# Edge matrix counted in steps of two tiles by 28 destination nodes, with the tile, degree and counting work pinned to the text's order

## Chip, cores and metric

The kernel runs on one core of one Trainium2 chip. The metric is the device time of one execution in microseconds (us), as the median of several runs. The engines are named as in the profile: PE (TensorE: matmuls, with PEld for their weight loads), DVE (VectorE), ACT (ScalarE), POOL (GpSimd) and SP (SyncE, which here only issues DMAs).

## What is computed

A graph of 6250 nodes and 100000 edges, sorted by destination `dst`, goes through two graph networks, each followed by a residual sum and a layer norm. Cut to what matters:

```
# network 0: three relational layers (R = 8 edge types, 128 features)
for l in range(3):
    h   = einsum('ni,rio->nro', x, weight[l])          # a message per node and type
    msg = h[src, etype] / max(count[dst, etype], 1)
    x   = segment_sum(msg, dst) + x @ root[l] + bias[l]
    if l < 2: x = relu(batch_norm(x))
x = layernorm(x_in + x)

# network 1: three steps of propagation over the same edges (64 features)
h = x @ W_in + b_in ;  deg = edges per src ;  dis = deg**-0.5 (0 where deg is 0)
acc = cur = h
for _ in range(3):
    cur = segment_sum(cur[dst] * dis[src] * dis[dst], src)
    acc = acc + cur
out = layernorm(x + (acc / 4) @ W_out + b_out)
```

## The kernel before, in words

**Gather stage.** The sorted edges form 782 tiles of 128. For each tile `one_sum` (L1046) lets POOL gather 128 message rows of 512 B by an indirect DMA (L1048) into one of 27 buffers `gt`, and PE multiplies them by a one-hot matrix `o` (L1051), which DVE makes for eight tiles at a time (`one_hots`, L1040 and L1042). `joined` lets DVE add a finished sum from PSUM into `agg` (L1630) or, for the low destinations, into `z` (L1079). Of each layer's 782 tiles, 92 are left to a dense product (`dense_sums`); 100 are gathered from node rows (`first_sums`, table `x_d`) and 590 from message rows (`window_sums`, table `h_d`): 690 gathers for each of three layers, 2070 in all. Between two layers stand a batch norm (L1674 to L1694), the writing of the new `x_d`, and 49 blocks of messages (`messages`, L953 to L958: PE, ACT, a DMA to `h_d`), which go on beside the next layer's first gathers.

**Side work.** Network 1 needs the number of edges between each pair of nodes, as a matrix, and the degrees. This is worked out beside the gathers by a generator, `side_work` (L1588), with N_SIDE steps: `hot_counts` (a small matrix for the low destinations), `degrees` (four tiles a step), and then `counts`. `take_turns` (L1615) moves the generator on in proportion to the gathered tiles: N_SIDE steps in TURNS = 1460 turns. With the code's constants N_SIDE is 1263, so a turn has 0.865 steps. No turn is taken in the dense stretch, in the first 66 tiles of layers 1 and 2 (the first 100 of layer 0), or in the last QUIET = 24 tiles of layers 0 and 1; after a batch norm FILL = 16 steps are put in at once (L1695).

**Counting.** `counts` (L1427) first lays out 245 steps: each holds four tiles whose destinations fall into one block of 128. It copies each step's edges into tables by one-hot matmuls (L1506). Then, for each of 980 tiles, DVE makes `row` (L1564), 1152 columns wide, with the value 16^field in the column of the edge's source, and, for four tiles at once, `dst_hot` (L1560), the one-hot of the destination. PE multiplies them into three PSUM banks of the pool `ps_w`, which has five (512, 512 and 128 columns, L1577; stationary `dst_hot`, moving `row`). Three instructions of `leave` (L1535) add the sum to that of the step before and store it as integers in `had`. SP writes `had` (576 KB) to the DRAM matrix `a_d` if the step is the last of its block (L1546, a conditional DMA).

**Last stage.** Network 1 (from L1711) reads `a_d` three times, in loads of 448 KB (L1829). DVE splits the nibbles (L1831, L1832), and PE multiplies by the features: 7203 matmuls (L1837).

**What sets the order.** A scheduler orders the instructions of each engine when the program is built. It goes by priorities from the text and by a model of durations, so an engine's order can differ from the text's. On the chip each engine runs its own order in sequence and waits on semaphores.

Of the kernel before, what the change touches and what calls it, by code (L numbers as in the profile page):

```python
# [519 lines left out]
def sorted_path(  # L520
# [34 lines left out]

    nc = tc.nc
# [48 lines left out]
    NG4 = Q * J // TS  # L605
    NST = NG4 + NBLK
# [6 lines left out]
    assert T1 + AND <= HT and P1 == 2 and W == 4 * P1 * P and 15 * NS1 <= NST * TS  # L613
    assert D == P and N * R <= 1 << 16 and R == 8 and H == 64
    assert 96 < Q <= P and N + P <= PAD and NBLK % CH == 0 and J == 2 * TS and NST <= 256
# [124 lines left out]
    b_out_r = const.tile([P, D], F32, name="b_out_r")  # L740

# [294 lines left out]
    def one_hots(column, share, width, t, end):  # L1036

        n = min(GPB, end - t)
        o = op.tile([P, GPB, HC], F32, name="o")
        nc.vector.tensor_tensor(o[:, :n, :width], iota_f[:, None, :width].to_broadcast([P, n, width]),  # L1040
                                column[:, t : t + n, None].to_broadcast([P, n, width]), op=OP.is_equal)
        nc.vector.tensor_tensor(o[:, :n, :width], o[:, :n, :width],  # L1042
                                share[:, t : t + n, None].to_broadcast([P, n, width]), op=OP.mult)
        return o

    def one_sum(pa, table, at, o, t, first_, last):  # L1046
        gt = gp.tile([P, D], F32, name="gt")
        nc.gpsimd.indirect_dma_start(  # L1048
            out=gt, out_offset=None, in_=table[:, :],
            in_offset=bass.IndirectOffsetOnAxis(ap=at[:, t : t + 1], axis=0))  # L1050
        nc.tensor.matmul(pa, gt, o, start=first_, stop=last)  # L1051
# [19 lines left out]
    def first_sums(l, nodes, steps, tiles, side):  # L1071
# [3 lines left out]
        def joined(t, pa):  # L1075
# [3 lines left out]
            nc.vector.tensor_add(to, to, pa.rearrange("p (d r) -> p d r", r=R))  # L1079
# [34 lines left out]
    ac = tc.alloc_tile_pool(name="ac", bufs=3)  # L1114
# [4 lines left out]
    a_d = dram.tile([NSL, P, NBLK, P], I32, name="a_d")  # L1119
    iota_c = kp.tile([P, S], mybir.dt.int16, name="iota_c")  # L1120
    nc.gpsimd.iota(iota_c, pattern=[[1, S]], base=0, channel_multiplier=0)
# [4 lines left out]
    nc.gpsimd.iota(iota_q, pattern=[[0, 1]], base=0, channel_multiplier=2,  # L1126
                   allow_small_or_imprecise_dtypes=True)

    e_src, e_rel, rel_s, e_val = (kp.tile([P, NST, TS], F32, name=f"e_tab{k}") for k in range(4))
# [10 lines left out]
    def hot_counts():  # L1140
# [130 lines left out]
        had = ac.tile([P, S], I32, name="had")  # L1271
        nc.vector.memset(had[:, :SR], 0)
        made, sums, at = {}, {}, {}
        for i in range(NS1 + 2):
            if i < NS1:
                hot = cp.tile([P, TS, P], BF16, name="dst_hot")
                nc.vector.tensor_tensor(hot[:, :P1, :], iota_f[:, None, :].to_broadcast([P, P1, P]),
                                        e_lo[:, i, :, None].to_broadcast([P, P1, P]), op=OP.is_equal)
                rows = []
                for j in range(P1):  # L1280
                    row = rp.tile([P, S], BF16, name="row")
                    nc.vector.tensor_scalar(row[:, :SR], iota_c[:, :SR], e_col[:, i, j : j + 1],
                                            e_v[:, i, j : j + 1], op0=OP.is_equal, op1=OP.mult)
# [3 lines left out]
            if 0 <= s < NS1:  # L1287
                hot, rows = made.pop(s)
                sums[s] = ps_w.tile([P, 512], F32, name="pw")
                for j in range(P1):  # L1290
                    nc.tensor.matmul(sums[s][:, :SR], hot[:, j, :], rows[j][:, :SR], start=(j == 0),
                                     stop=(j == P1 - 1))
            s = i - 2
            if s >= 0:
                now = ac.tile([P, S], I32, name="had")
                nc.vector.scalar_tensor_tensor(now[:, :SR], had[:, :SR], keep[:, s : s + 1],
                                               sums.pop(s)[:, :SR], op0=OP.mult, op1=OP.add)
# [7 lines left out]
                nc.sync.dma_start(c1_d[:, bass.ds(at[0, s], 1), :], now[:, None, :SR], cond=(at[1, s] == 1))  # L1305
# [82 lines left out]
    def degrees():  # L1388
# [9 lines left out]
        for t0 in range(0, NTS + TS, TS):  # L1398
            n = min(TS, NTS - t0)
            if n > 0:  # L1400
                hot = cp.tile([P, TS, P], BF16, name="lo_hot")
                blk = cp.tile([P, TS, NBLK], BF16, name="blk_hot")
                nc.vector.tensor_tensor(hot[:, :n, :], iota_f[:, None, :].to_broadcast([P, n, P]),  # L1403
                                        src_lo[:, t0 : t0 + n, None].to_broadcast([P, n, P]),
                                        op=OP.is_equal)
                nc.vector.tensor_tensor(blk[:, :n, :],
                                        iota_f[:, None, :NBLK].to_broadcast([P, n, NBLK]),
                                        src_blk[:, t0 : t0 + n, None].to_broadcast([P, n, NBLK]),
                                        op=OP.is_equal)
                made[t0] = hot, blk, n  # L1410
            if t0:
                hot, blk, n = made.pop(t0 - TS)
                for j in range(n):
                    t = t0 - TS + j
                    nc.tensor.matmul(pd, hot[:, j, :], blk[:, j, :], start=(t == 0), stop=(t == NTS - 1))  # L1415
# [11 lines left out]
    def counts():  # L1427

        B = NBLK
        edge = kp.tile([P, B], F32, name="edge")  # L1430
        nc.vector.tensor_scalar(edge, iota_f[:, :B], float(P), None, op0=OP.mult)
        d_in = dst_f[:, 1 : W + 1]
        p_t = [ps_w.tile([P, 512], F32, name="pw")[:B, :1] for _ in range(2)]
        for h in range(2):
            below = [cp.tile([Q, B], F32, name=f"below{k}") for k in range(2)]
            nc.vector.tensor_scalar(below[0], edge[:Q, :], d_in[:, h * 512 + 511 : h * 512 + 512], None,
                                    op0=OP.is_gt)
            nc.vector.tensor_scalar(below[1], edge[:Q, :], float(P), d_in[:, h * 512 : h * 512 + 1],
                                    op0=OP.add, op1=OP.is_gt)
            for k in range(2):  # L1440
                nc.tensor.matmul(p_t[k], below[k], ones[:Q, :1], start=(h == 0), stop=(h == 1))
        col = kp.tile([B, 8], F32, name="col")
        t0, n, incl, s0, delta, pos, top = (col[:, i : i + 1] for i in range(7))
        nc.vector.tensor_copy(t0, p_t[0])
# [477 lines left out]
```

## Time and profile before

| what | value |
|---|---|
| median of 11 runs | 3674.63 us (3664.24 to 3683.68) |
| the profiled execution's own time | 3665.64 us |
| its span, first to last instruction | 3663.9 us |
| busy: PE / DVE / POOL / ACT | 2889.7 / 2449.0 / 2152.0 / 321.1 us |
| DMA packets, bytes | 274421, 373.10 MB |
| last gather of layer 0; first gather of layer 1 | ends at 1026.5; starts at 1067.3 us |
| last gather of layer 2 | ends at 2968.8 us |
| last stage, L1837 | 7203 matmuls, 614.5 us busy |

Read it with the stages in mind: a share of the span is an average over stages with different limits. A group's line gives line, engine, operation, output<-input, shapes and count; behind the first bar the busy time and the mean of one in ns; behind the second the idle time of the engine just before them and what ended it. A line of a stretch gives, for each engine, the busy time in that stretch and, in brackets, the number of instructions, then the granted clock of PE, the DMA share and GB/s.

### The profile page before, as it was taken

The numbers are of one execution on the slowest core, as the hardware profiler recorded it, in microseconds if no ns is written. First come the engines' busy times: TensorE is split into PE (matmuls) and PEld (weight loads), VectorE is DVE, ScalarE is ACT, GpSimd is POOL, SyncE is SP. The second block draws the span as 40 slices with busy tenths as digits, with TensorE's granted clock in tenths as the row PEclk, the third lists the DMA queues.
The fourth block names the chain that finished last, engine by engine and source line by source line (L and its number), as shares of the span: only waits on it lengthen the run. The fifth ranks groups of instructions, "written<-read, shape, count | busy, mean of one in ns | idle before, by whom it ended". The sixth has DMA issues, their size and how long they took to land.

```text
span 3663.9 us, 51372 instructions
## 1 busy us (share of the span) xinstructions
PE 2889.7 (79%) x17520; PEld 2038.6 (56%) x17520; DVE 2449.0 (67%) x6315; ACT 321.1 (9%) x600; POOL 2152.0 (59%) x2083
## 2 busy tenths in 40 slices
PE   5865555687769878887767797787778769999998
PEld 3454444454444544444444454444445459999997
DVE  7667777873771688788548437878884557555555
ACT  3500000000016000000000340000001020000000
POOL 6677877777646777777766557777777730000000
PEclk9955555687769777677777897767878669999999
DMA  6611122233138222222422662222334224545442
GB/s 199 220 48 50 50 55 58 60 80 81 46 93 320 55 63 63 64 70 70 98 63 67 213 229 73 78 73 80 83 83 100 71 92 134 161 137 153 136 136 68
DMA packets 274421, 373.10 MB, mean 102 GB/s; under 512 B 86718, under 2 KB 197726, under 8 KB 274148
## 3 DMA queue, kind: packets, MB, share of 16 engines
q1 hardware_dynamic: 199464, 230.31, 20.0%
q0 software_dynamic: 66240, 135.79, 14.2%
q10 hardware_dynamic: 8444, 3.61, 0.4%
q8 instruction: 140, 2.29, 0.3%
q14 instruction: 133, 1.09, 0.1%
HBM read 250.74 MB, written 243.64 MB: 135 GB/s over the span
## 4 chain that ended last, share of the span: by engine, by line
PE 52%; DVE 25%; DMA 12%; issue 8%; POOL 2%; DVEq 1%; ACT 0%; POOLq 0%; ACTq 0%; SPq 0%
PE pw L1837 15%; PE ps L1051 12%; DMA gt<-h_d,gidx 10%; PE pw L1577 10%; DVE row L1564 6%; PE pw L956 6%; DVE had L1535 6%; PE pw L1352 3%; DVE agg L1630 2%; DVE o L1040 2%; POOL gt L1048 2%; PE pw L1379 1%; PE pw L969 1%; DVE dst_hot L1560 1%; DVE lo_hot L1403 1%
## 5 line engine op out<-in xcount | busy, mean ns | idle before, releaser
L1048 POOL DMA_INDIRECT gt<-h_d,gidx x1770 | 1830.5, 1034 | 561.7 <-issue 205.4
L1577 PE MATMUL pw<-row,dst_hot 128*128 128x128 bf16 (+1 forms) x2940 | 856.3, 418 | 298.7 <-DVE row L1564 146.1
L1051 PEld LDWEIGHTS ps<-o,gt 128*128 128x128 f32 x4140 | 781.4, 265 | 452.3 <-DMA gt<-h_d,gidx 189.3
L1051 PE MATMUL ps<-o,gt 128*128 128x48 f32 (+1 forms) x4140 | 811.0, 346 | 253.5 <-DMA gt<-h_d,gidx 155.5
L1564 DVE TENSOR_SCALAR row<-iota_c,e_tab,e_tab 128x1152 bf16<-128x1152 int16 x980 | 571.2, 591 | 280.2 <-PE pw L1577 278.6
L1577 PEld LDWEIGHTS <-dst_hot 128*128 128x128 bf16 x2940 | 340.5, 128 | 692.4 <-issue 610.5
L1837 PE MATMUL pw<-three,u 128*128 128x193 bf16 x7203 | 614.5, 248 | 14.4 <-DVE three L1764 10.1
L1837 PEld LDWEIGHTS <-u 128*128 128x128 fp8e3 x7203 | 601.3, 98 | 21.7 <-DVE three L1764 10.2
L1535 DVE SCALAR_TENSOR_TENSOR had<-had,keep,pw 128x128 int32<-128x128 int32 x735 | 444.0, 605 | 0.0
L1048 POOL DMA_INDIRECT gt<-x_d,xidx x200 | 195.8, 979 | 187.3 <-PE ps L1051 66.8
L956 PE MATMUL pw<-w,xT 128*128 128x512 f32 x588 | 285.8, 622 | 1.8 <-ACT hs L957 1.7
L1831 DVE TENSOR_SCALAR u<-packed 128x896 int32<-128x896 int32 x189 | 117.8, 624 | 194.2 <-PE pw L1837 194.1
L1403 DVE TENSOR_TENSOR lo_hot<-iota_f,e_tab 128x512 bf16<-128x512 f32 x196 | 134.7, 687 | 101.6 <-PE pd L1415 101.6
L1630 DVE TENSOR_TENSOR agg<-agg,ps 128x48 f32 x885 | 174.9, 198 | 32.0 <-PE ps L1051 26.7
L957 ACT COPY hs<-pw 128x512 f32<-128x512 f32 x294 | 168.7, 586 | 175.7 <-PE pw L956 144.3
L1040 DVE TENSOR_TENSOR o<-iota_f,lo 128x384 f32<-128x384 f32 x222 | 121.9, 549 | 87.7 <-PE ps L1051 87.6
L1352 PE MATMUL pw<-x,u 128*128 128x385 bf16 x735 | 169.1, 369 | 0.7 <-DVE x L1345 0.7
L1560 DVE TENSOR_TENSOR dst_hot<-iota_f,e_tab 128x512 bf16<-128x512 f32 x245 | 167.5, 684 | 0.0
L1048 POOL DMA_INDIRECT gt<-in_x_dram,xidx x100 | 122.7, 1227 | 67.8 <-PE ps L1051 37.5
L956 PEld LDWEIGHTS pw<-w,xT 128*128 128x128 f32 x588 | 106.8, 197 | 99.6 <-issue 80.9
L1079 DVE TENSOR_TENSOR z<-z,ps 128x56 f32 x300 | 61.9, 206 | 145.3 <-PE ps L1051 135.8
L1352 PEld LDWEIGHTS <-u 128*128 128x128 fp8e3 x882 | 97.4, 113 | 72.8 <-issue 29.5
(398 smaller groups left out, 1830.3 us busy)
## 6 DMA issues: line engine op xcount, KB each, us to landing
a_d<-had SPq DMA_DIRECT2D x245, 576.0 KB
packed<-a_d SPq DMA_DIRECT2D x189, 448.0 KB
h_d<-hs SPq DMA_DIRECT2D x147, 512.0 KB
gt<-h_d,gidx POOLq DMA_INDIRECT x1770
c_d<-had SPq DMA_DIRECT2D x62, 196.0 KB
packed<-c_d SPq DMA_DIRECT2D x21, 448.0 KB
x_d<-xc SPq DMA_DIRECT2D x24, 256.0 KB
xc<-in_x_dram SPq DMA_DIRECT2D x19, 256.0 KB
```

The lines of the kernel that those rows point to most:

```text
L956: nc.tensor.matmul(ph, xT[:, b * P : (b + 1) * P], w[:, c : c + 512], start=True, stop=True)
L1040: nc.vector.tensor_tensor(o[:, :n, :width], iota_f[:, None, :width].to_broadcast([P, n, width]), column[:, t : t + n, None].to_broadcast([ ...
L1048: nc.gpsimd.indirect_dma_start(out=gt, out_offset=None, in_=table[:, :], in_offset=bass.IndirectOffsetOnAxis(ap=at[:, t : t + 1], axis=0))
L1051: nc.tensor.matmul(pa, gt, o, start=first_, stop=last)
L1352: nc.tensor.matmul(sums[d][:, :C3D], us[d % 2][:, i, :, d // 2], x3[:, i, :], start=(c == 0 and i == 0), stop=(c * CH + i == NBLK - 1))
L1403: nc.vector.tensor_tensor(hot[:, :n, :], iota_f[:, None, :].to_broadcast([P, n, P]), src_lo[:, t0 : t0 + n, None].to_broadcast([P, n, P]), ...
L1535: nc.vector.scalar_tensor_tensor(now[:, c : c + w], had[:, c : c + w], keep[:, s : s + 1], p[:, :w], op0=OP.mult, op1=OP.add)
L1560: nc.vector.tensor_tensor(hots[s], iota_f[:, None, :].to_broadcast([P, TS, P]), rel_s[:, s, :, None].to_broadcast([P, TS, P]), op=OP.is_equal)
L1564: nc.vector.tensor_scalar(rows[i], iota_c, e_src[:, s, j : j + 1], e_val[:, s, j : j + 1], op0=OP.is_equal, op1=OP.mult)
L1577: nc.tensor.matmul(p[:, :w], hots[s][:, j, :], row[:, c : c + w], start=(j == 0), stop=(j == TS - 1))
L1630: nc.vector.tensor_add(to, to, pa)
L1837: nc.tensor.matmul(out_of(f), bytes_[f % 2][:, d, :, f // 2], cur[:, order[c0 + d], :], start=(c0 + d == 0 and f % 2 == 0), stop=(c0 + d = ...
```

## The change

**The counting step.** A step now holds two tiles (TU) whose destinations fall into one block of 28 nodes (DB); there are 224 such blocks (NDB), hence 616 steps and 1232 tiles. Stationary and moving operand change places. `row` is 252 columns wide (28 destinations by 9 residues of the source's block) and is the stationary side, in two halves of 126; the moving side is a one-hot of the source's place in its block of 128. So a tile needs two matmuls of 128 columns, a step one PSUM bank (126 x 256), one instruction in `leave`, and a write of 126 KB if it is the last of its block. N_SIDE becomes 1516 (1.038 steps a turn). The pools of `row` and `had` take smaller tiles; `had` has five buffers and not three.

**The tables** in `counts` are laid out for 616 steps, with twice as many one-hot matmuls of 308 columns, and for 224 blocks, in two halves of 112.

**The order.** `pin` ties an instruction to the one pinned before it on the same engine, without a semaphore: the scheduler must keep the text's order among them. Pinned are the one-hots `o`, the gather matmuls, the sums of `joined`, and the one-hots, rows, matmuls and `had` of hot_counts, degrees and counts. The rest stays free: messages, batch norm, dense sums, table building, DMAs.

**The last stage** reads the matrix in its new layout: per load one residue of block numbers (6 or 5 blocks), 512 B in a piece and not 3584 B: 243 loads, not 189, of 384 or 320 KB. The matmuls are as many and as large as before.

```diff
     TS = 4
-    NG4 = Q * J // TS
-    NST = NG4 + NBLK
+    TU = 2
+    DB = 28
+    NDB = NP // DB
+    HB = DB * NSL // 2
+    NST = Q * J // TU + NDB
...
+    in_turn = {}
+
+    def pin(ins):
+
+        last = in_turn.get(ins.ins.engine)
+        if last is not None:
+            tc.add_manual_dep(ins.ins, last.name,
+                              mybir.DependencyInfo(mybir.DependencyClass.NoSync, mybir.DependencyReason.DATA),
+                              reason="order of turns")
+        in_turn[ins.ins.engine] = ins.ins
...
-        nc.tensor.matmul(pa, gt, o, start=first_, stop=last)
+        pin(nc.tensor.matmul(pa, gt, o, start=first_, stop=last))
...
-    ac = tc.alloc_tile_pool(name="ac", bufs=3)
+    ac = tc.alloc_tile_pool(name="ac", bufs=5)
...
-    a_d = dram.tile([NSL, P, NBLK, P], I32, name="a_d")
+    a_d = dram.tile([NDB, 2 * HB, P], I32, name="a_d")
...
-                nc.tensor.matmul(pd, hot[:, j, :], blk[:, j, :], start=(t == 0), stop=(t == NTS - 1))
+                pin(nc.tensor.matmul(pd, hot[:, j, :], blk[:, j, :], start=(t == 0), stop=(t == NTS - 1)))
...
-            for j in range(TS):
-                pe = ps_w.tile([P, 512], F32, name="pw")
-                for h in range(2):
-                    c = h * 512 + j * P
-                    nc.tensor.matmul(pe[:, :NST], of[:, c : c + P], sel[h], start=(h == 0), stop=(h == 1))
-                nc.vector.tensor_copy(to[:, :, j], pe[:, :NST])
+            for j in range(TU):
+                for x0 in range(0, NST, NSH):
+                    pe = ps_w.tile([P, 512], F32, name="pw")
+                    for h in range(4):
+                        c = (h * TU + j) * P
+                        nc.tensor.matmul(pe[:, :NSH], of[:, c : c + P], sel[h][:, x0 : x0 + NSH],
+                                         start=(h == 0), stop=(h == 3))
+                    nc.vector.tensor_copy(to[:, x0 : x0 + NSH, j], pe[:, :NSH])
...
-            s, k, p, had, now = left.pop(0)
-            c, w = pieces[k]
-            nc.vector.scalar_tensor_tensor(now[:, c : c + w], had[:, c : c + w], keep[:, s : s + 1],
-                                           p[:, :w], op0=OP.mult, op1=OP.add)
+            s, p, had, now = left.pop(0)
+            pin(nc.vector.scalar_tensor_tensor(now[:HB, : 2 * P], had[:HB, : 2 * P], keep[:HB, s : s + 1],
+                                           p[:HB, : 2 * P], op0=OP.mult, op1=OP.add))
...
-                rows[i] = rp.tile([P, S], BF16, name="row")
-                nc.vector.tensor_scalar(rows[i], iota_c, e_src[:, s, j : j + 1], e_val[:, s, j : j + 1],
-                                        op0=OP.is_equal, op1=OP.mult)
+                rows[i] = rp.tile([P, SR], BF16, name="row")
+                pin(nc.vector.tensor_scalar(rows[i][:, : 2 * HB], iota_c[:, : 2 * HB], e_col[:, s, j : j + 1],
+                                        e_val[:, s, j : j + 1], op0=OP.is_equal, op1=OP.mult))
...
-            for (c, w), p in zip(pieces, pa):
-                nc.tensor.matmul(p[:, :w], hots[s][:, j, :], row[:, c : c + w], start=(j == 0),
-                                 stop=(j == TS - 1))
+            for c in range(2):
+                pin(nc.tensor.matmul(sums[s][:HB, c * P : (c + 1) * P], row[:, c * HB : (c + 1) * HB],
+                                 hots[u // TS][:, u % TS, :], start=(j == 0 and c == 0), stop=(j == TU - 1 and c == 1)))
...
-            for c0 in range(0, NBLK, CH):
-                packed = ap_.tile([P, CH, P], I32, name="packed")
-                nc.sync.dma_start(packed, a_d[sl, :, c0 : c0 + CH, :])
+            for c0 in range(NSL):
+                blocks = list(range(c0, NBLK, NSL))
+                m = len(blocks)
+                packed = ap_.tile([P, FLD, P], I32, name="packed")
+                nc.sync.dma_start(packed[:, :m, :], a_rows[:, c0::NSL, sl, :])
```

## The prediction

> **What bounds the kernel now.** I read the page's groups first: they say what counting costs each engine. The columns behind the first bar are busy us and mean ns, behind the second idle us.
>
> ```profile
> L1048 POOL DMA_INDIRECT gt<-h_d,gidx x1770 | 1830.5, 1034 | 561.7 <-issue 205.4 <-DMA gt<-h_d,gidx 142.6 <-PE ps L1051 119.5
> L1577 PE MATMUL pw<-row,dst_hot 128*128 128x512 bf16 x1960 | 750.7, 502 | 67.4 <-DVE had L1535 64.2 <-DVE xc L1693 2.2 <-DMA gt<-h_d,gidx 0.5
> L1564 DVE TENSOR_SCALAR row<-iota_c,e_tab,e_tab 128x1152 bf16<-128x1152 int16 x980 | 571.2, 591 | 280.2 <-PE pw L1577 278.6
> L1535 DVE SCALAR_TENSOR_TENSOR had<-had,keep,pw 128x512 int32<-128x512 int32 x490 | 361.5, 739 | 0.0
> L1577 PE MATMUL pw<-row,dst_hot 128*128 128x128 bf16 x980 | 230.9, 250 | 231.2 <-DVE row L1564 146.1 <-DVE had L1535 78.4 <-DMA gt<-h_d,gidx 2.0
> L1560 DVE TENSOR_TENSOR dst_hot<-iota_f,e_tab 128x512 bf16<-128x512 f32 x245 | 167.5, 684 | 0.0
> L1535 DVE SCALAR_TENSOR_TENSOR had<-had,keep,pw 128x128 int32<-128x128 int32 x245 | 82.8, 338 | 0.0
> L1282 DVE TENSOR_SCALAR row<-iota_c,e_tab 128x392 bf16<-128x392 int16 x124 | 42.0, 380 | 0.0
> ```
>
> So counting takes 982 us of PE and 1183 us of DVE. Whether that is on the path, the stretches tell (degrees at 400; counting at 1300, 1400, 2500; last stage at 3200):
>
> ```profile
> 400.00:500.00 100.00, 55.52 (x344) 43.87 (x343) 72.87 (x199) 0.00 (x0) 79.44 (x68) 0.50 0.20 53
> ...
> 1300.00:1400.00 100.00, 78.56 (x337) 46.46 (x336) 82.76 (x189) 0.00 (x0) 76.84 (x77) 0.73 0.23 62
> 1400.00:1500.00 100.00, 84.47 (x341) 50.49 (x341) 78.65 (x177) 0.00 (x0) 76.84 (x77) 0.65 0.25 67
> ...
> 2500.00:2600.00 100.00, 77.85 (x364) 45.65 (x363) 86.53 (x197) 0.00 (x0) 77.15 (x76) 0.79 0.29 80
> 3200.00:3300.00 100.00, 100.00 (x1198) 99.80 (x1197) 50.77 (x121) 4.03 (x8) 0.00 (x0) 1.00 0.47 136
> ```
>
> In counting, PE (78 to 84 of 100 us) and DVE (79 to 87) are not full, and POOL does 76 or 77 gathers every time. POOL's timeline says why, here in counting and then near the end, where nothing else runs:
>
> ```profile
> 1440.09 0.94 POOL L1048 DMA_INDIRECT gt<-h_d,gidx  x1 [0.30 <-DMA gt<-h_d,gidx]
> 1441.34 1.31 POOL L1048 DMA_INDIRECT gt<-h_d,gidx  x1 [0.30 <-issue]
> 1442.95 0.94 POOL L1048 DMA_INDIRECT gt<-h_d,gidx  x1 [0.31 <-DMA gt<-h_d,gidx]
> ```
> ```profile
> 2950.37 0.94 POOL L1048 DMA_INDIRECT gt<-h_d,gidx  x1 [0.30 <-issue]
> 2951.62 0.94 POOL L1048 DMA_INDIRECT gt<-h_d,gidx  x1 [0.30 <-issue]
> ```
>
> Every gather has 0.30 us of idle time ahead of it, whatever the releaser: POOL never waits longer for a buffer. A gather costs 0.94 + 0.30 = 1.25 us undisturbed, about 1.31 us in counting. **The gather stage is bound by POOL's issue**, and the chain of waits, which names PE and DVE there, hops between engines that only keep pace. From 3062 us on PE is full and bounds the last stage. In between POOL stands still only at the layers' ends, 40.8 us after layer 0 and 41.5 after layer 1.
>
> **The change part by part, against the profiled execution's 3665.6 us (span 3663.9).**
>
> *DVE.* `row`: the rows of 1152 columns (591 ns) and 392 (380) give 0.278 ns a column, so 252 columns take 380 - 140 x 0.278 = 341 ns; 1232 of them 420 us (571 before). `had`: from 338 ns at 128 columns and 739 at 512, 256 columns take 472; 616 make 291 us (444). `dst_hot` keeps its 684 ns, 308 times: 211 us (168). Sum 922 us, 261 less.
>
> *PE.* 2464 matmuls of 128 columns, at the 250 ns of that form, are 616 us, 366 less.
>
> *What of it is on the path?* Neither sum, since POOL covers both: in the stretch from 1300 a gather's 1.30 us hold 1.07 us of DVE (82.76 over 77) and 1.02 us of PE (78.56 over 77). Their relief counts in three places.
>
> (1) *POOL's instructions become shorter.* The stretches of 100 us from 700, 1200 to 1800, 1900, and 2200 to 2800 hold 1059 gathers in 1070.5 us of busy POOL, 1.01 each; undisturbed it is 0.94. These 70 ns, 74 us in all, come while DVE works. If the excess goes with DVE's counting time (922/1183) it falls by 16 us; if with the rows' columns (1232 x 252 against 980 x 1152) by 54; if with the number of instructions (1232/980) it grows by 19. I take -25, nearest to the first. The Trainium skill, "SBUF — State Buffer", "Who interferes with whom", says that a tensor_scalar in a two-port mode locks GpSimd out for its whole length. The trace agrees in part: the gather of 1.31 us above ran while DVE made rows. By that rule `row` alone would count, 571 to 420 us, and the term would be about -20 (74 x 151/571).
>
> (2) *The layers' ends.* Layer 0's last gather ends at 1026.5, but the batch norm's first instruction starts at 1039.9: DVE is still busy with rows, `had` and one-hots, scheduled among the last sums. Landing (2.5 us), matmul pair (0.66) and some joins (0.2 each) need about 4. Less counting, and none mixed in by the pinned order, may save 9 each; I take 7, so -14 (0 to -18).
>
> (3) *The fill.* Its 16 steps take 14.2 us of PE between 1060 and 1100 (9.69 + 4.46 in stretches of L1577 alone), holding three of five `ps_w` banks a step. The messages need such banks too and begin at 1088.4, though their input is complete at 1058.8. Then PE is full to 1197 and POOL stutters. New fill: 32 matmuls, at most 8 us, one bank a step. I take -12 a layer, -24. The 100 gathers beside it need 125 us of POOL and take 148 and 152, so -50 is the end; +10 the other, if the fill's pinned DVE work (12 us) delays the first one-hots.
>
> *What is added.* Table building: 32 matmuls of 308 columns for 16 of 245 (a record of that kind took 379 to 554 ns, two a matmul), and 20 for 5: some 40 us of PE more, in twelve steps. The 27 gather buffers, 34 us of gathers, hide it; without cover +25. SP: 616 conditional writes, 73 ns when skipped. 224 writes of 126 KB replace 49 of 576: the same bytes.
>
> *Last stage.* PE's 7203 matmuls stay. DMA: 24192 packets of 3584 B (192 ns each) become 169344 of 512 B; 101822 packets of that size took 28.6 ns on average, so 16 engines need 303 us for 290 before, inside 580 us of PE. DVE gets 108 instructions more, each shorter: 249 us for 235, at 51% busy. I take +3 (0 to +15).
>
> Sum: -25 - 14 - 24 + 3 = -60, or **3606 us** against 3665.6. The median of the runs shown is 9 us above the profiled execution, so **3615 us** on its scale.
>
> **Rivals** (median scale).
>
> *A. The text's order makes DVE the bound: slower.* A pinned `row` waits for its buffer, which PE frees only after a gather has landed; rows, `had` and joins queue behind it on DVE. In degrees each turn now brings 1.038 steps, not 0.865: DVE's 1.07 us a gather (72.87/68) become about 1.24, of 1.47 available. In counting I get (0.341 + 0.171 + 0.236) x 1.038 + 0.25 = 1.03 us, of 1.27. It decides if the round trip costs over 0.24 us each turn, beyond what the three tiles of lead hide. At 0.32 us a turn, (0.32 - 0.24) x 1460 turns = +117, the 60 us are lost too, and the time is **3790**; at 0.40, +234. For: DVE waits 278.6 us for PE at `row`. Against: lead 3, 27 gather buffers. 14%.
> The Trainium skill, "TensorE: Matmul & The Clock Gate", "What's actually happening", adds that an idle PE falls back to half its clock. The trace agrees: 0.50 granted at 400 us, where PE is 56% busy. Even so it kept up there, 344 matmuls in 55.5 us, 0.161 each; new counting needs 4.1 a turn, 0.66 us. So the rule alone makes no bound.
>
> *B. POOL hides all of it.* The excess stays, and the layers' ends stay as they are: **3675**, within 0.2%. For: 0.30 us everywhere. Against: DVE 89% busy from 1020 to 1040. 13%.
>
> *C. The pins don't reorder what matters.* Messages and dense sums are free, so the scheduler may still put fill ahead of messages; only (1) and part of (2) remain: **3645**. 17%.
>
> *D. Small packets bind the last stage.* At twice 28.6 ns, 606 us of DMA for 580 of PE, and each slice starts late: +30 to +60, less 60: **3660**; at three times, 3950. Against: bursts of 1151 packets in 2 us (28 ns). 6%.
>
> *Forecast*, with all three terms: 50%, its own range 3550 to 3645.
>
> **Numbers.** The range needs C, B and the near side of A and D, and the ends of (1) to (3): **3550 to 3705**; outside are A's far part (11%), D's (3%) and a larger gain (6%). This kernel's measurement can tell about 0.2%, 7 us. Faster: 0.50 + 0.17 + 0.03 of B and D: 0.70. Same: 0.10 from B, D. Slower: A and the rest, 0.20.
>
> **What would show it.** (1): POOL's mean for `h_d` below 1.034 us, about 1.02. POOL still with 0.30 ahead of each gather; if more than a few have over 0.6, A. (2): batch norm 5 to 8 us after the last gather. (3): messages begin before 1080 in layer 1. Costs: `row` near 341 ns, `had` 472, matmuls of the last stage at 85 ns apart. Wrong if counting was on the path after all: then far more than 60 us go.

## The result and the profile after

The changed kernel takes **3580.47 us** (median of 8 runs, 3576.95 to 3584.33); beside it the kernel before took 3671.23 us (31 runs). The ratio is 0.9752, 95% interval [0.9741, 0.9762]: 2.5% faster, and 35 us below the forecast of 3615. The profiled execution has a span of 3575.2 us, 88.7 us less than the 3663.9 of before.

The groups of the changed kernel, as those shown of before: behind the first bar busy us and mean ns, behind the second idle us and releasers.

```profile
L1064 POOL DMA_INDIRECT gt<-h_d,gidx x1770 | 1796.0, 1015 | 552.8 <-issue 230.4 <-DMA gt<-h_d,gidx 114.6 <-PE pw L1601 114.3
L1587 DVE TENSOR_SCALAR row<-iota_c,e_tab,e_tab 128x252 bf16<-128x252 int16 x1232 | 420.9, 350 | 322.8 <-PE pw L1601 321.7
L1601 PE MATMUL pw<-dst_hot,row 128*126 128x128 bf16 x2464 | 412.0, 318 | 56.9 <-DVE row L1587 53.2 <-DVE xc L1718 3.0
L1560 DVE SCALAR_TENSOR_TENSOR had<-had,keep,pw 126x256 int32<-126x256 int32 x616 | 292.2, 474 | 1.6 <-PE pw L1601 1.6
L1583 DVE TENSOR_TENSOR dst_hot<-iota_f,e_tab 128x512 bf16<-128x512 f32 x308 | 211.2, 686 | 0.0
```

Counting now costs DVE 924 us (420.9 + 292.2 + 211.2) and PE 412. Four of the stretches of 100 us as before:

```profile
400.00:500.00 100.00, 65.22 (x392) 48.46 (x392) 90.28 (x240) 0.00 (x0) 78.67 (x71) 0.50 0.20 56
1300.00:1400.00 100.00, 68.07 (x321) 55.98 (x321) 68.31 (x200) 0.00 (x0) 76.23 (x79) 0.50 0.26 68
2500.00:2600.00 100.00, 66.62 (x310) 54.61 (x310) 67.94 (x200) 0.00 (x0) 76.74 (x77) 0.50 0.30 78
3200.00:3300.00 100.00, 100.00 (x1199) 100.00 (x1197) 58.30 (x147) 4.85 (x10) 0.00 (x0) 1.00 0.53 151
```

PE and DVE fell to 67 to 69 of 100 us in counting, and POOL does only one or two gathers more in the same time, 79 for 77 from 1300 us: relief of engines that only kept pace is worth little by itself. POOL's timeline has the same 0.30 us ahead of a gather:

```profile
1302.08 0.94 POOL L1064 DMA_INDIRECT gt<-h_d,gidx  x1 [0.30 <-DMA gt<-h_d,gidx]
```

At the end of layer 0, the timeline shows the last gather, the last joins, one late row and the batch norm's first instruction, 4.8 us after the gather's end (13.4 before); then layer 1's first finished message, 30 us sooner than the 1090.3 of before. First the changed kernel, then the kernel before:

```profile
1024.03 0.94 POOL L1064 DMA_INDIRECT gt<-h_d,gidx  x1 [0.30 <-issue]
...
1027.95 1.64 DVE L1655 TENSOR_TENSOR agg<-agg,ps 128x48 f32 x7 [16.29 <-PE ps L1067]
1029.51 0.34 DVE L1587 TENSOR_SCALAR row<-iota_c,e_tab,e_tab 128x252 bf16<-128x252 int16 x1
1029.77 1.87 DVE L1699 BATCH_NORM_STATS2 st<-agg 128x6 f32<-128x512 f32 x3
...
1060.82 0.58 ACT L973 COPY hs<-pw 128x512 f32<-128x512 f32 x1 [2.62 <-PE pw L972]
```
```profile
1025.52 0.95 POOL L1048 DMA_INDIRECT gt<-h_d,gidx  x1 [0.30 <-PE ps L1051]
...
1039.89 7.39 DVE L1674 BATCH_NORM_STATS2 st<-agg 128x6 f32<-128x512 f32 x13
...
1090.26 0.58 ACT L957 COPY hs<-pw 128x512 f32<-128x512 f32 x1 [21.58 <-PE pw L956]
```

**Where the time went**, by stages that POOL's gathers bound: from the first to the last gather of a kind, with the pauses between layers. Three experiments stand beside it; each column is a single profiled execution. "Order" is the pinned text's order, "fill" the 16 side steps after each batch norm. "Gathers' time above 0.943 each" is what POOL's 2070 gather instructions took beyond the 0.943 us of an undisturbed one.

| stage, us | before | before + order | before, no fill | changed | changed, no order |
|---|---|---|---|---|---|
| layer 0, node gathers | 183.4 | 189.7 | 188.0 | 191.7 | 185.2 |
| layer 0, message gathers | 832.7 | 804.5 | 832.6 | 822.9 | 901.5 |
| pause after layer 0 | 40.8 | 32.0 | 41.3 | 31.6 | 43.0 |
| layer 1, node gathers | 148.5 | 135.5 | 126.9 | 129.5 | 130.4 |
| layer 1, message gathers | 783.1 | 782.6 | 786.7 | 761.5 | 972.6 |
| pause after layer 1 | 41.5 | 32.9 | 47.2 | 33.0 | 43.0 |
| layer 2, node gathers | 152.3 | 127.2 | 130.0 | 134.8 | 138.6 |
| wait for messages of layer 2 | 0.3 | 64.8 | 0.3 | 0.3 | 0.3 |
| layer 2, message gathers | 775.5 | 781.0 | 773.1 | 763.5 | 963.3 |
| after the last gather | 695.1 | 699.6 | 696.1 | 695.7 | 699.1 |
| span | 3663.9 | 3660.9 | 3633.1 | 3575.2 | 4087.9 |
| gathers' time above 0.943 each | 197.0 | 189.7 | 194.7 | 160.6 | 161.7 |

### The profile page after: what moved, and what is told of

Its sections match the earlier page's. It is cut to its first block, busy times and chain, and to the rows that moved or that the text cites. A ratio compares the mean times of both kernels' runs of the same rounds, so it can differ in the third digit from the quotient of the medians.

```text
span 3575.2 us, 53292 instructions
## 1 busy us (share of the span) xinstructions
PE 2711.8 (76%) x17110; PEld 2165.9 (61%) x17110; DVE 2273.9 (64%) x6623; ACT 324.2 (9%) x600; POOL 2115.3 (59%) x2083
## 3 DMA queue, kind: packets, MB, share of 16 engines
q14 instruction: 155, 1.27, 0.1%
## 4 chain that ended last, share of the span: by engine, by line
PE 41%; DMA 32%; DVE 11%; issue 10%; POOL 5%; DVEq 0%; ACT 0%; POOLq 0%; SPq 0%; ACTq 0%
DMA gt<-h_d,gidx 32%; PE pw L1865 15%; PE ps L1067 8%; PE pw L972 7%; POOL gt L1064 5%; PE pw L1368 3%; PE pw L1601 2%; DVE row L1587 1%; DVE had L1560 1%; PE pw L1395 1%; PE pw L985 1%; DVE dst_hot L1583 1%; DVE agg L1655 1%; PE ps L1823 1%; PE pd L1368 1%
## 5 line engine op out<-in xcount | busy, mean ns | idle before, releaser
L1064 POOL DMA_INDIRECT gt<-h_d,gidx x1770 | 1796.0, 1015 | 552.8 <-issue 230.4
L1067 PE MATMUL ps<-o,gt 128*128 128x48 f32 (+1 forms) x4140 | 1148.5, 391 | 660.2 <-DMA gt<-h_d,gidx 579.0
L1067 PEld LDWEIGHTS ps<-o,gt 128*128 128x128 f32 x4140 | 948.1, 291 | 946.3 <-DMA gt<-h_d,gidx 773.4
L1587 DVE TENSOR_SCALAR row<-iota_c,e_tab,e_tab 128x252 bf16<-128x252 int16 x1232 | 420.9, 350 | 322.8 <-PE pw L1601 321.7
L1601 PE MATMUL pw<-dst_hot,row 128*126 128x128 bf16 x2464 | 412.0, 318 | 56.9 <-DVE row L1587 53.2
L1601 PEld LDWEIGHTS <-row 128*126 128x126 bf16 x2464 | 337.0, 225 | 74.5 <-DVE row L1587 64.5
L1560 DVE SCALAR_TENSOR_TENSOR had<-had,keep,pw 126x256 int32<-126x256 int32 x616 | 292.2, 474 | 1.6 <-PE pw L1601 1.6
L1064 POOL DMA_INDIRECT gt<-x_d,xidx x200 | 195.3, 976 | 133.6 <-PE pw L1601 33.4
L1859 DVE TENSOR_SCALAR u<-packed 128x640 int32<-128x640 int32 (+1 forms) x243 | 126.7, 521 | 201.8 <-PE pw L1865 199.1
L1583 DVE TENSOR_TENSOR dst_hot<-iota_f,e_tab 128x512 bf16<-128x512 f32 x308 | 211.2, 686 | 0.0
L1368 PE MATMUL pw<-x,u 128*128 128x385 bf16 x735 | 178.8, 385 | 7.1 <-DVE x L1361 3.6
L1368 PEld LDWEIGHTS <-u 128*128 128x128 fp8e3 x882 | 100.8, 119 | 80.2 <-issue 39.5
```

The costliest lines, as they stand in the source:

```text
L1064: nc.gpsimd.indirect_dma_start(out=gt, out_offset=None, in_=table[:, :], in_offset=bass.IndirectOffsetOnAxis(ap=at[:, t : t + 1], axis=0))
L1067: pin(nc.tensor.matmul(pa, gt, o, start=first_, stop=last))
L1368: nc.tensor.matmul(sums[d][:, :C3D], us[d % 2][:, i, :, d // 2], x3[:, i, :], start=(c == 0 and i == 0), stop=(c * CH + i == NBLK - 1))
L1560: pin(nc.vector.scalar_tensor_tensor(now[:HB, : 2 * P], had[:HB, : 2 * P], keep[:HB, s : s + 1], p[:HB, : 2 * P], op0=OP.mult, op1=OP.add))
L1583: pin(nc.vector.tensor_tensor(hots[i // TS], iota_f[:, None, :].to_broadcast([P, TS, P]), flat(e_lo)[:, i : i + TS, None].to_broadcast([P, ...
L1587: pin(nc.vector.tensor_scalar(rows[i][:, : 2 * HB], iota_c[:, : 2 * HB], e_col[:, s, j : j + 1], e_val[:, s, j : j + 1], op0=OP.is_equal, ...
```

## Experiments

**1. The changed kernel without the text's order.**

```diff
     in_turn = {}
+    PINNED = False
...
-        if last is not None:
+        if last is not None and PINNED:
```

> The changed kernel with no instruction pinned: the new counting step alone, in the scheduler's own order. Theory (the smaller step gives most of the gain, the order little): gathers' excess over 0.943 us falls to about 165 us as in the changed kernel, the messages of layers 1 and 2 still begin early, the stall of 13.7 us behind the table building and the longer first stage (191.7 us) are gone, but the batch norm starts later behind the last gather than 4.8 us: 3570 to 3600 us. Rival (the text's order gives most): the layers' ends and the fill stay as in the kernel before, 3630 to 3660 us.

Measured 4088.59 us, 1.1129 of before [1.1107, 1.1151]. Neither theory had that. The stretches of this kernel show how it comes about; the second lies after the gathers of layer 1 had stopped, and the next line is the gather that ends the stop:

```profile
1500.00:1600.00 100.00, 56.08 (x226) 45.49 (x224) 37.32 (x118) 0.00 (x0) 76.07 (x79) 0.50 0.23 60
1940.00:2040.00 100.00, 36.83 (x216) 26.87 (x216) 69.44 (x188) 0.00 (x0) 0.00 (x0) 0.50 0.10 26
```
```profile
2157.38 0.95 POOL L1065 DMA_INDIRECT gt<-h_d,gidx  x1 [220.48 <-PE ps L1068]
```

POOL runs at its own pace, 79 gathers in 100 us, but only 34 rows were made in the stretch from 1500, where the changed kernel makes 80. Left free, the scheduler puts several gather sums between two counting steps: from 1500 us PE has 12 to 20 matmuls of gather sums between every four of counting, where the changed kernel has four. The steps left over stand between the last of these sums and the layer's dense stretch, with the remaining sums behind both. So counting runs alone (107 rows in the 100 us from 1940, POOL at 0), the dense product follows, and POOL waits 220 us for a sum to free a buffer. The same happens in layer 2 (211 us) and, smaller, in layer 0 (62 us). The order is no addition to the new step; the new step needs it.

**2. The kernel before with the text's order** on the same instructions, its own counting step kept.

```diff
-        nc.tensor.matmul(pa, gt, o, start=first_, stop=last)
+        pin(nc.tensor.matmul(pa, gt, o, start=first_, stop=last))
```

> The kernel before, with its old step of four tiles by 128 destinations, but with the same kinds of instructions pinned to the text's order. Theory (the step gives most): the gathers' excess stays near 197 us, the fill still holds the messages back (148 and 152 us from the first gather of a layer's node rows to the last), only the batch norm comes earlier and the two stalls in the dense stretch (13 and 10 us) may go: 3640 to 3665 us. Rival (the order gives most): 3590 to 3620 us.

Measured 3656.41 us, 0.9957 [0.9945, 0.9969], as the theory said, though for reasons it did not have. By the table the order alone shortens both pauses as much as the whole change does (to 32.0 and 32.9 us), shortens the node gathers of layers 1 and 2 by 13 and 25 us and layer 0's message gathers by 28, and ends the stalls of 12.9 and 9.3 us that POOL had in the dense stretches of layers 0 and 1. It then loses 64.8 us in one place. Without that loss the order alone would stand near 3596 us in the profile (3660.9 less 64.5, an estimate), so much of the change's 88.7 us might be had without the new step; no run tried it. The timeline of POOL:

```profile
2114.55 0.95 POOL L1059 DMA_INDIRECT gt<-x_d,xidx  x1 [0.30 <-issue]
2180.34 0.94 POOL L1059 DMA_INDIRECT gt<-h_d,gidx  x1 [64.83 <-DMA xc<-in_x_dram]
```

The message matmuls of this kernel (L967) in stretches of 20 us tell the rest; the columns are PE, PEld, clock, DMA share and GB/s:

```profile
2060.00:2080.00 20.00, 8.21 (x8) 2.10 (x8) 0.50 0.34 105
2080.00:2100.00 20.00, 9.40 (x10) 2.65 (x10) 0.50 0.33 102
2100.00:2120.00 20.00, 16.41 (x33) 5.33 (x32) 0.92 0.79 283
```

The messages are not pinned, and the scheduler spread them among the pinned gather sums, 8 in 20 us where 33 fit. Of 196 message matmuls of the layer 126 were left when the node gathers were over (at 2115.5 us), and the message gathers, which read their result, stood until 2180. In the changed kernel layer 2's messages are done by 2080, before the node gathers end.

**3. The kernel before without the fill.**

```diff
-    FILL = 16
+    FILL = 0
```

> The kernel before with FILL = 0: no side steps right behind a batch norm. Theory (the fill's matmuls and its three banks a step hold the messages back): the messages of layers 1 and 2 begin about 15 us earlier behind the batch norm, the 100 gathers beside them take 130 to 135 us for 148 and 152, POOL's stutter there goes, and the time falls by 25 to 40 us, to 3630 to 3646 us. Rival (the messages are held back by something else): the stretch stays at 148 and 152 us and the time within 7 us of 3671.

Measured 3638.61 us, 0.9912 [0.9885, 0.9940]: as the theory said. Layer 1's first finished message comes at 1066.5 us:

```profile
1066.52 0.59 ACT L957 COPY hs<-pw 128x512 f32<-128x512 f32 x1 [1.83 <-PE pw L956]
```

The node gathers of layers 1 and 2 shorten by 21.6 and 22.3 us, the other stages stay within 6. So the hold was the fill's. In layer 1, experiment 2 ends 13.0 of the 21.6 us with the fill in place, and experiment 1, without any order but with a step of one bank, 18.1 (130.4 us; 138.6 in layer 2): either part of the change is enough for most of this term.

**4. Time between the tables and the first counting step.**

```diff
         nc.vector.tensor_scalar(low, low, 23, None, op0=OP.logical_shift_left)
         yield
+        for _ in range(24):
+            yield
```

> The changed kernel with 24 empty side steps between the table building and the first counting step (N_SIDE 24 larger). Theory (the first pinned counting matmul waits for the tables and holds up the gather matmuls pinned behind it until the 27 buffers are full): POOL's stall of 13.7 us at 651 us goes, nothing else changes: 3580 - 14 = 3567 us. Rival (the tables' matmuls and DVE work themselves are too much for that place): the stall stays over 8 us, the time within 5 us of 3580.

Measured 3584.69 us, 0.9755 [0.9736, 0.9775]: no gain. The changed kernel has one stall here: DVE works on the tables (L1544 to L1549) in a row up to 648.7 us, the first row comes behind them, PE's next gather sum behind that row, and POOL runs out of buffers:

```profile
639.69 5.87 DVE L1544 SCALAR_TENSOR_TENSOR e_tab<-e_tab,e_tab 128x1232 f32<-128x1232 f32 x4
...
649.15 0.73 PE L1601 MATMUL pw<-dst_hot,row 128*126 128x128 bf16 x4 [16.30 <-DVE row L1587]
...
650.55 1.45 POOL L1064 DMA_INDIRECT gt<-h_d,gidx  x1 [13.70 <-PE ps L1067]
```

With the empty steps the stall is gone, and gathers beside the tables are longer:

```profile
648.61 1.18 POOL L1064 DMA_INDIRECT gt<-h_d,gidx  x1 [0.30 <-DMA gt<-h_d,gidx]
```

Over layer 0's message gathers the time above 0.943 us rose from 73.6 to 90.8 us, the stalls fell from 13.4 to 0, and the stage went from 822.9 to 826.7. Only part of the rise lies beside the tables (3.4 to 10.5 us); 7.5 us of it lie in degrees (53.6 to 61.1), where the kernel of experiment 11, which keeps a stall of 12.3 us at the tables, has 60.5. So removing the stall gained nothing here, and that the gathers lengthen because it is gone is not shown.

**Two other chips.** Experiments 5 to 8 shared a chip on which the kernel before took 4352.69 us, experiments 9 and 10 (and the first run of 11) one where it took 4270.60; what differs there is told at the end. The expected times do not apply to them. They are compared within their group, by rows, stages and the gathers' lengths.

**5 and 6. The order on one engine alone.**

```diff
+        if ins.ins.engine != ET.PE:
+            return
         last = in_turn.get(ins.ins.engine)
```

Experiment 6 has ET.DVE in that line.

> The changed kernel with the text's order kept on TensorE alone; VectorE's order is left free. Theory (without the order, counting matmuls stand behind gather sums on TensorE, their row buffers stay full, and the steps left over run alone at the layer's end): TensorE's order is what matters, 3575 to 3640 us, about 81 rows made in each 100 us of counting. Rival (VectorE's order matters, because the joining of a sum or the making of a row stands behind the other kind there): 3850 to 4090 us, 34 to 60 rows in 100 us.

> The changed kernel with the text's order kept on VectorE alone; TensorE's order is left free. Theory (TensorE's order matters): 3850 to 4090 us, with a stretch of counting alone at the layer's end. Rival (VectorE's order matters): 3575 to 3640 us. Second rival (the order of either engine forces the other's, since each row waits for a matmul and each matmul for a row): this and the kernel with TensorE's order alone are both at 3575 to 3640 us.

Measured 4148.39 and 4215.85 us; experiment 7, with both engines in order from the message gathers on, took 4034.41. The rows of counting in one stretch, for order on PE, on DVE and on both:

```profile
1800.00:1900.00 100.00, 24.01 (x67) 0.50 0.22 59
```
```profile
1800.00:1900.00 100.00, 22.52 (x67) 0.50 0.21 56
```
```profile
1800.00:1900.00 100.00, 23.76 (x69) 0.50 0.24 62
```

Counting keeps its rate in both, and no stretch of counting alone appears: POOL's longest wait for a sum inside a layer's message gathers is 37 and 30 us, against 220 in experiment 1. So the mechanism of the second rival holds: the order of either engine forces most of the other's. Its times do not: it expected the full order's time, and the free engine costs 2.8% (PE's order kept) and 4.5% (DVE's) beside experiment 7 on this chip. On the usual one neither was tried.

**7. No order in layer 0's node gathers.** There the changed kernel had lost 8.3 us: late in that stage 32 message matmuls stand in a row on PE, where the kernel before has 20.

```diff
+        if not pinning[0]:
+            return
         last = in_turn.get(ins.ins.engine)
...
     for _ in other_tiles:
         pass
+    pinning[0] = True
```

> The changed kernel without the text's order in the first layer's node gathers, where 33 message matmuls in a row held the gathers back. Theory: the 8 us that this stage lost come back and stay, 3570 to 3575 us, the stage at 182 to 186 us instead of 191.7. Rival: the time comes back in the same layer's counting, which then starts with less done, 3578 to 3583 us.

Measured 4034.41 us. The stage took 196.5 us, 8.9 less than the 205.4 of experiment 8, which keeps the order there. Experiments 5 and 6 tell which engine's order does it: with PE's order alone the stage takes 195.3 us and the messages stand as in the free kernel, with DVE's alone it takes 203.7 and they stand as in the changed one. The total can't be told on this chip; experiment 11 takes it up.

Part of the 8.3 us may be scatter. On the usual chip four kernels (before and experiments 1, 3 and 11) have the same order of messages on PE in this stage, and it took them 183.4, 185.2, 188.0 and 187.3 us; with the order it took 189.7 to 191.7 (experiments 2 and 4 and the changed kernel).

**8. Rows three times as wide.**

```diff
+    WR = 6 * HB
...
-                rows[i] = rp.tile([P, SR], BF16, name="row")
-                pin(nc.vector.tensor_scalar(rows[i][:, : 2 * HB], iota_c[:, : 2 * HB], e_col[:, s, j : j + 1],
+                rows[i] = rp.tile([P, WR], BF16, name="row")
+                pin(nc.vector.tensor_scalar(rows[i], iota_c, e_col[:, s, j : j + 1],
```

> The changed kernel with each counting row made 756 columns wide, of which the matmuls read the first 252: VectorE writes three times as much and nothing else changes. Rows of 1152 columns lengthened the gathers beside them by some 0.13 to 0.165 us per us of their own time, those of 252 columns by about 0.01. Theory (the lengthening goes with the columns moved): the gathers' time above 0.943 us each rises by 40 to 60 us, from 161, and the kernel is at 3620 to 3645 us. Rival 1 (it goes with VectorE's busy time alone, at a share of 0.15): some 25 us more, 3600 to 3612 us. Rival 2 (it goes with the number of instructions): no more than 5 us, 3578 to 3588 us.

Measured 4041.24 us. One more line differs that is not shown: `had` has three buffers here, not five, and its effect was not tried apart. POOL's and the rows' groups, of experiment 7 and then of this kernel:

```profile
L1067 POOL DMA_INDIRECT gt<-h_d,gidx x1770 | 1807.2, 1021 | 911.9 <-issue 361.1 <-PE ps L1070 235.9 <-PE pw L1605 148.0
L1591 DVE TENSOR_SCALAR row<-iota_c,e_tab,e_tab 128x252 bf16<-128x252 int16 x1232 | 423.6, 355 | 670.7 <-remote 462.3 <-PE ps L1070 107.3 <-PE pw L1605 82.0
```
```profile
L1065 POOL DMA_INDIRECT gt<-h_d,gidx x1770 | 1857.3, 1049 | 849.1 <-issue 362.4 <-PE ps L1068 203.0 <-PE pw L1602 132.8
L1588 DVE TENSOR_SCALAR row<-iota_c,e_tab,e_tab 128x756 bf16<-128x756 int16 x1232 | 580.2, 482 | 510.8 <-remote 356.3 <-PE ps L1068 68.2 <-PE pw L1602 60.6
```

The gathers' time above 0.943 us rose by 52.6 us (170.7 to 223.3), 50.1 of it in the message gathers from the first row on (62.1 to 112.2). That is inside the theory's 40 to 60 and twice what DVE's 157 us more would give at 0.15, so the prices of both rivals fail: a row's width counts for more than its share of time. That the lengthening goes with the columns alone is not shown. Experiment 2's kernel moves 1.13 million columns in its rows and this one 0.93 million, with the same excess in the message gathers of layers 1 and 2, 88.6 and 89.5 us (53.3 in the changed kernel). The kernel's total hardly moved, since on this chip POOL waits often and longer gathers eat the waits: those above 0.31 us in the message gathers fell from 370 to 309 us. So the expected times were not tested.

**9. One `dst_hot` for all steps.** This leaves out 307 of the 308 one-hots, so the counts are not those of the graph. They also decide which path the kernel ends with, so it runs its general path behind the last stage as well, 14864.97 us in all; only the stages before that are read.

```diff
-                if i % TS == 0:
+                if i % TS == 0 and i > 0:
+                    hots[i // TS] = hots[0]
+                elif i == 0:
```

> The changed kernel with the counting's dst_hot (686 ns, one for every four tiles) built for the first four tiles of the step loop alone and read by all the others; the 307 later ones are left out. Theory (a VectorE instruction lengthens a gather beside it according to its kind: dst_hot by 0.16 to 0.25 us for each us of its own time, the rows by 0.01): the gathers' time above 0.943 us each falls by 34 to 53 us from 161, and the kernel is at 3528 to 3547 us. Rival (the lengthening comes from the transfers in flight or from instructions that read PSUM, and dst_hot only runs at the same times): it falls by less than 10 us, 3570 to 3582 us.

POOL's group, here and then in experiment 10 on the same chip:

```profile
L1064 POOL DMA_INDIRECT gt<-h_d,gidx x1770 | 1777.5, 1004 | 933.5 <-issue 368.4 <-PE ps L1067 263.1 <-PE pw L1603 148.0
```
```profile
L1064 POOL DMA_INDIRECT gt<-h_d,gidx x1770 | 1814.2, 1025 | 886.6 <-issue 359.0 <-PE ps L1067 252.0 <-PE pw L1602 109.1
```

The gathers' time above 0.943 us in the 2070 gathers was 136.6 us, against 177.3 in experiment 10: 40.7 less, inside the theory's 34 to 53. In the message gathers beside counting, where the edit acts, it fell by 33.4 (66.0 to 32.6), or 0.16 us for each us of `dst_hot`; beside the kernel of experiment 11 on this chip (73.5) it is 40.9, or 0.19. So `dst_hot` is about half of what the change left there, and the theory holds; the kernel's own time says nothing of it.

**10. `dst_hot` compared in bf16.**

```diff
-                    pin(nc.vector.tensor_tensor(hots[i // TS], iota_f[:, None, :].to_broadcast([P, TS, P]),
-                                            flat(e_lo)[:, i : i + TS, None].to_broadcast([P, TS, P]),
+                    pin(nc.vector.tensor_tensor(hots[i // TS], iota_b[:, None, :].to_broadcast([P, TS, P]),
+                                            lo_b[:, i : i + TS, None].to_broadcast([P, TS, P]),
```

> The changed kernel with dst_hot compared in bf16 (numbers under 128, exact in it) in place of float32. Theory (the lengthening of gathers goes with dst_hot's time, and bf16 operands make it shorter): its 686 ns become 300 to 450 ns, the gathers' time above 0.943 us each falls by 12 to 30 us, 3550 to 3569 us. Rival 1 (with two-byte operands it holds GpSimd off for more of its time, whatever its length): the gathers get longer by 10 to 50 us, 3590 to 3630 us. Rival 2 (its time stays, as the broadcast operands are read one at a time): no change, 3576 to 3585 us.

Measured 4018.42 us (before: 4270.60). Its group:

```profile
L1584 DVE TENSOR_TENSOR dst_hot<-iota_b,e_tab 128x512 bf16<-128x512 bf16 x308 | 211.2, 686 | 0.0
```

The second rival: 686 ns as in float32. The gathers' 177.3 us above 0.943 each, against 160.6 in the changed kernel, would fit the first rival too, but experiment 11's kernel, with `dst_hot` in float32, has 183.0 on this same chip. So no effect shows, and this run is taken to stand for the unchanged new kernel on its chip, where that kernel itself was not run.

**11. No order in layer 0's node gathers, and no fill.**

```diff
-    FILL = 16
+    FILL = 0
```

The line is changed in the kernel of experiment 7.

> The changed kernel without the text's order in the first layer's node gathers, and without the 16 side steps put after each batch norm; the two edits act in different stages. Theory (in the kernel before, the side steps held the messages of layers 1 and 2 back, and taking them away there gave 33 us; in the changed kernel that hold is gone already): the first stage falls from 191.7 to 182-188 us, the third layer's node gathers from 134.8 to 126-130 us, the second's stay within 3 us of 129.5, 3563 to 3574 us in all. Rival (the side steps still cost what they did): 20 to 30 us less than that, 3540 to 3560 us, with messages starting more than 8 us earlier after batch norm in both layers.

> The same kernel as in the run before with the two edits (no text's order in the first layer's node gathers, no side steps after batch norm), wanted on a chip where SyncE's register instructions take their usual 0.04 us. Theory: the first stage falls by 4 to 9 us and keeps it, the other stages stay, 3568 to 3577 us, 0.971 to 0.9745 of the kernel before. Rival (what the first stage gains is lost in the counting behind it, which starts at another point): 3578 to 3585 us, 0.9745 to 0.9765.

On the chip of experiments 9 and 10: 4015.31 us, 0.9432 of before [0.9381, 0.9482], against 0.9424 [0.9371, 0.9478] of experiment 10, so no difference. On a chip where the kernel before took 3669.91 us: **3574.86 us**, 0.9738 [0.9725, 0.9752]. The interval overlaps that of the changed kernel (0.9741 to 0.9762), so a gain of some 5 us is possible and not shown. The time lies in the theory's range (3568 to 3577); the stages of the profiled execution, the longest of the five (3582.26 us, span 3580.5), go as the rival had it: layer 0's node gathers fell from 191.7 to 187.3 us, its message gathers rose from 822.9 to 827.7. Which of the two holds is open. The node gathers of layers 1 and 2 are 126.9 and 133.9 us (129.5 and 134.8), so the fill costs the changed kernel little: most of the hold of experiment 3 was gone.

## Why the prediction was right, and where it was off

The forecast's sum was -60 us on the profiled execution; measured were -88.7. All three mechanisms were there. What was mis-sized, and what was left out ("excess" is the gathers' time above 0.943 us each):

| term | predicted | measured | how |
|---|---|---|---|
| (1) excess beside counting | -25 | -26.3 | message gathers from the first row on, 96.2 to 69.9 |
| excess of all other gathers | not costed | -10.1 | 100.8 to 90.7 |
| (2) layers' ends | -14 | -17.8 | pauses 40.8 and 41.5 to 31.6 and 33.0 |
| (3) fill | -24 | -36.5 | node gathers of layers 1 and 2 |
| stalls in dense stretches | not costed | -22.2 | 12.9 and 9.3 us at 936 and 1911, now none |
| table building | 0, behind 27 buffers | +13.4 | stall at 651 us |
| layer 0's node gathers | not costed | +8.3 | messages in a row, part may be scatter (experiment 7) |
| last stage | +3 | +0.6 | 695.1 to 695.7 |

The rows overlap by a few us (excess of node gathers is in their stages too); they add up to -90.6, for -88.7. Of the 28.7 us beyond the forecast, 22.2 come from stalls that it did not have: "In between POOL stands still only at the layers' ends" overlooked two, of which this is the longer.

```profile
936.47 1.46 POOL L1048 DMA_INDIRECT gt<-h_d,gidx  x1 [13.21 <-PE ps L1051]
```

The order ends both (experiment 2). The three terms themselves gave 80.6 us for the 63 forecast; 21.7 us lost and 32.3 gained elsewhere were not in the sum. So it is in part luck that the total came as near as it did.

**Term (1)** was right in its own place: its 74 us are an excess beside counting, and there 26.3 us went. That the choice among three ends, nearest to DVE's time (-16), hit it so closely is in part luck. Experiments 8 and 9 show two things at work: wider rows lengthen gathers by more than their added time at 0.15, and `dst_hot` by 0.16 to 0.19 us per us. The narrower rows gave much and the 63 more one-hots took some back. The Trainium skill, "SBUF — State Buffer", "Who interferes with whom", says that a tensor_scalar in a two-port mode locks GpSimd out for its whole length if it was issued first. By that rule the prediction had -20 from `row` alone. The direction fits experiment 8, the size doesn't: that sum leaves 54 us to the rows of 252 columns, and in experiment 9, without `dst_hot`, everything beside counting leaves 32.6. The 10.1 us of the other gathers lie where no counting runs; in degrees alone the changed kernel and experiments 4 and 11 scatter from 53.6 to 61.1 us.

**Term (2)** was right in mechanism and nearly in size. Experiments 1 and 2 show that it is the order's alone: pauses of 43.0 us without it, 32.0 and 32.9 with it.

**Term (3)**: right in place and cause, as experiment 3 shows. The size, 12 us a layer, was taken near the fill's 14.2 us of PE and far from the end of -50; measured are 19.0 and 17.5. POOL's waits above 0.30 us a gather beside the messages were 20 and 24 us in layers 1 and 2, and are 0 and 9 now.

**The step that failed outright** is "The 27 gather buffers, 34 us of gathers, hide it". They hide work on other engines, but not 33 us in which PE makes no gather sum: from 617 us it makes the tables' own matmuls, up to 633, and then waits 16.3 us, up to 649.2, for a row that stands behind the tables on DVE. The stated price without cover was +25; it was 13.4, and in experiment 4 removing the stall gained nothing.

**Rival A** failed: DVE is at 90% in degrees (1.27 us of busy time a gather; 1.24 was forecast), and POOL still has its 0.30. TensorE's clock did fall, to 0.50 granted in the counting stretches shown (0.65 to 0.79 before), and PE kept up at 68%, as the prediction argued. The gather sums got longer, though: 391 ns a matmul and 1148.5 us of PE, against 337 ns and 895.1 us in experiment 2, which has the same order at 0.71 to 0.79. That is over half of what counting gave back on PE; that the clock is the cause is likely, not shown. (Counting had 856.3 us of PE before, by the page: the prediction's 982 adds two forms that overlap. Its 616 for the new step came out as 412.0.) **Rival B** fell with the shorter gathers. **Rival C** had the order weak; experiments 1 and 2 show the reverse. The prediction credited the new step with terms (1) and (3); by itself, in the scheduler's order, that step costs 11%. **Rival D** failed: the last stage is 0.6 us longer, at a DMA share of 0.48 for 0.45 from its first matmul to its last.

## What to carry to other kernels

In a stage bound by one engine's issue, cheaper work on the others is worth what it takes off that engine's instructions and ends, so look for both before you add up busy times. When work is made smaller, look at the order that the scheduler gives it: the same instructions, left free, cost 500 us here by arriving late. An order that is written out for some instructions also moves those that stay free, so look at these in each layer.

## What was not expected of the hardware

**SyncE's register instructions.** On the two chips of experiments 5 to 10 the kernel before took 19 and 16% longer than on the others, and experiment 10, which stands for the changed kernel, 12%, with nearly the same durations of rows (354 ns for 350), `had` (473 for 474) and gathers (1025 for 1015). The difference found in the traces is on SyncE. A few of its records around one conditional write of `a_d`, start us, duration us, operation; first in the changed kernel, then in experiment 10:

```
1457.66 0.33 DMA_DIRECT2D      1456.51 0.33 DMA_DIRECT2D
1458.03 0.04 ALU_OP            1456.88 0.04 ALU_OP
1458.10 0.04 ALU_OP            1457.17 0.71 ALU_OP
1458.17 0.05 FUSED_REGOPS      1457.89 0.01 FUSED_REGOPS
```

Between 1200 and 3000 us, 9 of SyncE's 2576 register and semaphore instructions took over 0.4 us in the changed kernel, all of them semaphore instructions; in experiment 10 it was 363 of 2455, 271 of them register instructions, most near 0.70, with 417 gaps of 0.60 to 0.80 us between instructions (32 in the changed kernel). SyncE issues the writes that free `had` and the message buffers, so DVE then waits for a releaser that the profile calls "remote" (455 us at `row`) and PE behind it. That these slow instructions are the cause is argued from the traces, not shown, and why they are slow there stays open. The last stage, 639 to 642 us from its first to its last matmul, is as long on all chips.
